# Layer 2 of a four-layer image kernel: high and low parts in the layout of the images, columns reordered by the evictions, another order of steps

## The chip, the cores and the metric

The kernel runs on one core of one Trainium2 chip. The metric is the time of one execution on the device, in microseconds (us). Before the change three runs took 6418.2, 6427.65 and 6427.76 us, so the median is 6427.65 us.

## The reference

The input is a batch of 32 images with 96 channels of 56 x 56. Four layers follow each other, and each adds its result to its input. Every layer first normalises its input over groups of three channels (`_gn`). The change lies in layer 2, a block with weights and activations rounded to four bits:

```python
def _L2_conv_ref(x, w1, ..., v3):
    h = bn(conv(x, quant_w(w1, BITW), b1, 1, 0, 1), g1, be1, m1, v1)      # 96 -> 576 channels, 1x1
    h = act_q(h, BITA)                                                    # clip to [0, 1], round to 15ths
    h = bn(conv(h, quant_w(w2, BITW), b2, 1, 1, HID), g2, be2, m2, v2)    # 3x3 in each channel
    h = act_q(h, BITA)
    h = bn(conv(h, quant_w(w3, BITW), b3, 1, 0, 1), g3, be3, m3, v3)      # 576 -> 96 channels, 1x1
    return x + h

x = x + _L2_conv_ref(_gn(x), ...)
```

The other layers are an inverted residual block with squeeze and excitation (layer 0), a wavelet convolution (layer 1) and a 9 x 9 convolution in each channel (layer 3). They aren't touched.

## The kernel before

**Layout.** Between the layers an image lies as 96 partitions (channels) with 3136 values each, in the order tile, phase, row, column: four tiles `t` of 14 rows; in each tile four phases `p`, which are the columns with the same remainder by 4; then 14 rows, then 14 columns `q`. Two images share one buffer `pair`, so an image `xt` is read in runs of 14 values (56 bytes) with a gap after each. Layers 1 and 3 work in this layout. Layer 2's 3x3 convolution needs columns that are neighbours to lie beside each other ("natural" order).

**Work of one image in layer 2.** The 576 hidden channels are five blocks `k` of 128 (the last one holds 64 channels, each in two halves). Each step has a letter, and the numbers after it are its arguments:

- `s`, `u`, `v`, `b`, `x` make the statistics and centre the image (VectorE, called DVE in the profile, and two tiny matmuls `pn` and `pv`).
- `h` (`high`, line 1011) writes `hi`, the normalised image in the rounded format that TensorE multiplies (F32R), on ScalarE (ACT). `l` (`low`, line 1017) writes `lo`, what that rounding left, on DVE. Both go from the layout of the phases to natural order, so they write one value in four: `h` once for each of four phases, `l` once for each of four phases in each of four tiles.
- `e` (`expand`, line 1039) multiplies block `k` of the first weights with tile `i` of `hi` and of `lo`: two halves of 392 columns, two matmuls each. The eviction (line 1029 on ACT, 1027 on DVE) scales the sum and writes it as whole numbers, `u`.
- `m` (`activate`, line 1048, DVE) clips `u` into the padded image `apad`.
- `a` (`depthwise`, line 1058) does the nine taps as matmuls of 64 x 64 with diagonal weights, four to an area of the array: 72 matmuls for each `k` and half image (36 for the last block). It fills two PSUM tiles (one for the last block). Their evictions (lines 1029 and 1027) put the columns back in the order of the phases.
- `n` (line 1048, DVE) clips, `j` (`project`, line 1095) multiplies with the third weights, `d` (line 1102, DVE) adds to the image, `o` takes the statistics for layer 3 and stores the images.
- `r` (line 1022, DVE) prepares the sum with the input.

**Order.** The queues of TensorE (PE), DVE and ACT are in program order, which is written out by hand: `run_steps` goes through the string `L2_ORDER` once for each image, and a `+` or `-` after a step means the next image or the one before. `L2_ON_DVE` names the evictions that go to DVE: `e00` is `expand` for `k` = 0, `i` = 0, and `a301` is the second PSUM tile of `depthwise` for `k` = 3, first half. In the order before, an image's expansions, mixed with the projections of the image before it, are followed by all of its depthwise steps. The issue of DMAs on SP and the one power on POOL (line 989) are not ordered by hand.

**Buffers.** All sums of layer 2, `ps`, `pn`, `pv`, `psd` and `psj`, are tiles of one pool with four buffers of two PSUM banks each. `hi` and `lo` have one buffer, `u` three. Three pairs of images are held; after the second image of a pair, `store` writes it to `y2` and `fetch` loads the next pair from `y1` into its place, 112 bytes to a packet.

Of the kernel before, what the change touches and what calls it, by code (L numbers as in the profile page):

```python
# [12 lines left out]
F32R = mybir.dt.float32r  # L13
I16 = mybir.dt.int16
AF = mybir.ActivationFunctionType
ALU = mybir.AluOpType
# [4 lines left out]
B, C, H, W = 32, 96, 56, 56  # L21
# [4 lines left out]
RT = 7  # L26
NT = RT * W
W2 = W // 2
NPH = 4
W4 = W // NPH  # L30
HH = H // 2
PH = HH * NPH
NP = H // (2 * RT)
# [31 lines left out]
    z1 t28 c0 a2  # L65
"""
L2_ORDER = """
    e00 e10 e11 e12 l3 j0- d0- e01 e20 e02 e21 r u+ e03 e13 j1- m0 e22 d1- e30 m1 e40 v+ j2- d2- e31
    e41 e23 b+ e42 j3- x+ e32 e33 m2 d3- m3 s++ e43 h0+ m4 a00 a10 o- a11 n1 a01 a20 h1+ a30 a21 l0+
    a31 n0 a40 l1+ n2 l2+ a41 n3 n4  # L70
"""
L2_ON_DVE = {"e00", "e20", "a301", "a201"}


class Shared:
# [843 lines left out]
def layer2(ctx, tc, S, k2, y1, y2, norm3):  # L919
# [9 lines left out]
    nc = tc.nc  # L929
    cp = ctx.enter_context(tc.tile_pool(name="l2d", bufs=1))  # L930
    pool = ctx.enter_context(tc.tile_pool(name="l2", bufs=1))
# [4 lines left out]
    CC, HALF, N9 = NBLK - 1, 64, 2 * NBLK - 1  # L936
    w1, w3, diag, s1, o1, s2, o2, s3, o3 = k2.constants
# [59 lines left out]

        nc.vector.tensor_scalar(im["xt"], im["xt"], im["gm"], None, ALU.subtract)

    def natural(t, p):  # L1000

        return t.rearrange("c (t r) (q p) -> c p t r q", t=NP, p=NPH)[:, p]

    def phase(im, p):
        return im["xt"].rearrange("c (t p r) q -> c p t r q", t=NP, p=NPH)[:, p]

    def high(im, half):
        if half == 0:
            im["hi"] = pool.tile([C, H, W], F32R, tag="hi", name="hi")
        for p in (2 * half, 2 * half + 1):  # L1010
            nc.scalar.activation(natural(im["hi"], p), phase(im, p), AF.Copy, scale=im["rstd"])  # L1011

    def low(im, i):
        if i == 0:
            im["lo"] = pool.tile([C, H, W], F32R, tag="lo", name="lo")
        for p in range(NPH):
            nc.vector.scalar_tensor_tensor(natural(im["lo"], p)[:, i], phase(im, p)[:, i], im["rstd"],
                                           natural(im["hi"], p)[:, i], ALU.mult, ALU.subtract)

    def residual(im):  # L1020

# [2 lines left out]
    def evict(out, ps, s, o, c, on_dve):  # L1024

        if on_dve:
            nc.vector.tensor_scalar(out, ps, s[:, c : c + 1], o[:, c : c + 1], ALU.mult, ALU.add)
        else:
            nc.scalar.activation(out, ps, AF.Identity, bias=o[:, c : c + 1], scale=s[:, c : c + 1])  # L1029

    def expand(im, k, i):

        if i == 0:
            im["u"][k] = up.tile([128, HW], I16, tag="u", name="u")
        ps = psum.tile([128, 2, 512], F32, tag="mm", name="ps")
        for j in range(2):
            r0 = (2 * i + j) * RT
            for part in ("hi", "lo"):
                nc.tensor.matmul(  # L1039
                    ps[:, j, :NT], w1[:, k * 128 : k * 128 + 128],  # L1040
                    im[part][:, r0 : r0 + RT, :].rearrange("c h w -> c (h w)"),
                    start=(part == "hi"), stop=(part == "lo"),
                )
        evict(im["u"][k][:, 2 * i * NT : 2 * (i + 1) * NT].rearrange("p (j n) -> p j n", j=2), ps[:, :, :NT],
              s1, o1, k if k < CC else N9 - 1, f"e{k}{i}" in L2_ON_DVE)

    def clip(out, u):
        nc.vector.tensor_scalar(out, u, 0.0, 15.0, ALU.max, ALU.min)
# [12 lines left out]
    def depthwise(im, k, h):  # L1061
# [21 lines left out]
        for x, (n, p, c) in enumerate(parts):  # L1083
            evict(u[:, 2 * n * NT : 2 * (n + 1) * NT].rearrange("p (m j x) -> p j m x", j=2, m=NPH),
                  p[:, :, :NT].rearrange("p j (x m) -> p j m x", m=NPH), s2, o2, c, f"a{k}{h}{x}" in L2_ON_DVE)

# [20 lines left out]
    def store(im):  # L1107
# [7 lines left out]
    step = {  # L1115
        "s": stats, "u": group_mean, "v": group_variance, "b": residual_factors, "x": centre,
        "h": high, "l": low, "r": residual, "e": expand, "m": activate, "a": depthwise, "n": activate2,
        "j": project, "d": add, "o": store,
    }
# [115 lines left out]
def kernel_body(tc, w, x, out):  # L1235
    nc = tc.nc
    with ExitStack() as ctx:
# [33 lines left out]
        with ExitStack() as ctx2:  # L1271
            k2 = Layer2(ctx2, tc, S, w, y1)

            def behind(pair):
                k2.prepare(pair)
                if not k2.stages:
                    k2.begin(min(2 * pair, C - GR))

            layer1(tc, w, y0, norm1, t1, t2, t3, y1, behind)
            k2.begin(C)  # L1280
            layer2(tc, S, k2, y1, y2, norm3)
# [122 lines left out]
```

## Time and profile before

| | |
|---|---|
| median of three runs | 6427.65 us |
| the profiled execution: time, span | 6420.77 us, 6419.0 us |
| clock of TensorE granted, mean | 0.975 |
| layer 2, first expansion to last projection | 4212.2 to 5949.6 us |
| busy in that stretch: PE, DVE, ACT | 1620, 1207, 1213 of 1737 us |
| DMA issues in layer 2 | 392 KB each, six to a pair of images and direction |

How to read it. The profile is of one execution. A busy time is the sum of an engine's instructions. In the tables of groups a row has the line of the code, the engine, the operation, what it writes and reads with shapes, the count, and then busy time in us, the mean of one in ns, and the idle time before it with what ended it. In a timeline the columns are start in us, duration in us, engine, line, operation, and in brackets how long the engine had been idle and what released it; "issue" means that nothing in the profile explains it. In the table of waits a row ends with the time in total, the number of waits and the longest.

### The profile page before, as it was taken

The numbers are of one execution on the slowest core, as the hardware profiler recorded it, in microseconds if no ns is written. First come the engines' busy times: TensorE is split into PE (matmuls) and PEld (weight loads), VectorE is DVE, ScalarE is ACT, GpSimd is POOL, SyncE is SP. The second block draws the span as 40 slices with busy tenths as digits, with TensorE's granted clock in tenths as the row PEclk, the third lists the DMA queues.
The fourth block names the chain that finished last, engine by engine and source line by source line (L and its number), as shares of the span: only waits on it lengthen the run. The fifth ranks groups of instructions, "written<-read, shape, count | busy, mean of one in ns | idle before, by whom it ended". The sixth has DMA issues, their size and how long they took to land.

```text
span 6419.0 us, 115759 instructions
## 1 busy us (share of the span) xinstructions
PE 6013.8 (94%) x49064; PEld 3571.1 (56%) x49064; DVE 5173.8 (81%) x5533; ACT 4052.9 (63%) x5716; POOL 223.1 (3%) x157
## 2 busy tenths in 40 slices
PE   4999999999999999999969999989999999999699
PEld 2444444444444444444435666668777777777344
DVE  6999999999999999999947666667676766776587
ACT  4676666766766667667535566567676766766355
POOL 4000000000000000000000000000000000000000
PEclk8999999999999999999979999999999999999899
DMA  3022221222211222113365866558787686964988
GB/s 95 6 48 53 45 46 32 49 55 47 42 32 43 54 49 42 32 37 40 23 86 142 150 148 146 130 30 54 39 53 41 51 43 44 51 42 29 174 254 245
DMA packets 1305765, 452.95 MB, mean 71 GB/s; under 512 B 1123151, under 2 KB 1301063, under 8 KB 1303327
## 3 DMA queue, kind: packets, MB, share of 16 engines
q1 hardware_dynamic: 1305246, 445.54, 47.5%
q8 instruction: 386, 6.32, 0.5%
q14 instruction: 133, 1.08, 0.1%
HBM read 284.44 MB, written 214.08 MB: 78 GB/s over the span
## 4 chain that ended last, share of the span: by engine, by line
PE 76%; ACT 13%; DVE 5%; DMA 3%; issue 2%; POOL 1%; SPq 1%; ACTq 0%; DVEq 0%; POOLq 0%
PE psd L388 18%; PE psd L1058 11%; PE ps L335 11%; PE ps L1039 6%; PE pc L774 6%; PE pc L1210 5%; PE psj L447 5%; ACT junk L287 4%; DVE h L360 4%; PE psj L1095 3%; ACT hi L1011 2%; ACT hpad L347 2%; PE pc L758 2%; ACT a L1029 2%; PE psj L448 2%
## 5 line engine op out<-in xcount | busy, mean ns | idle before, releaser
L360 DVE SCALAR_TENSOR_TENSOR h<-hpad,l_wdw,h 128x3136 f32<-128x3136 f32 x768 | 2662.6, 3481 | 40.7 <-ACT h L355 26.8
L1058 PE MATMUL psd<-apad,diag 64*64 64x392 bf16 x20736 | 930.3, 332 | 117.1 <-issue 62.4
L335 PE MATMUL ps<-xn,l_wexp 96*128 96x392 f32 x2560 | 894.5, 501 | 32.6 <-ACT xn L321 31.5
L1058 PEld LDWEIGHTS <-diag 64*64 64x64 bf16 x20736 | 699.3, 107 | 343.7 <-issue 170.3
L388 PE MATMUL psd<-hpad,diag 64*64 64x392 f32 x9216 | 831.1, 511 | 0.0
L347 ACT ACTIVATE hpad<-ps,o,s 128x784 f32<-128x784 f32 x512 | 546.6, 1082 | 305.0 <-PE ps L335 301.8
L335 PEld LDWEIGHTS ps<-xn,l_wexp 96*128 96x128 f32 x2560 | 479.4, 191 | 401.7 <-issue 37.3
L604 ACT COPY T<-raw 32x112 f32<-32x112 f32 (+2 forms) x1440 | 462.8, 384 | 300.4 <-DMA raw<-tdiff 216.8
L1029 ACT ACTIVATE u<-ps,o,s 128x784 int16<-128x784 f32 x576 | 536.9, 1003 | 160.6 <-PE ps L1039 141.7
L1029 ACT ACTIVATE a<-psd,o,s 128x784 int16<-128x784 f32 x448 | 424.6, 1000 | 322.2 <-PE psd L1058 322.2
L447 PE MATMUL psj<-h,wg 128*96 128x392 f32 x1536 | 606.7, 531 | 15.3 <-ACT hpad L347 7.7
L388 PEld LDWEIGHTS psd<-hpad,diag 64*64 64x64 f32 x9216 | 346.9, 131 | 467.9 <-issue 433.3
L1039 PE MATMUL ps<-hi,l_w1q 96*128 96x392 f32 x1280 | 462.5, 361 | 9.3 <-ACT hi L1011 9.2
L1210 PE MATMUL pc<-x,T 128*112 128x416 f32 (+1 forms) x1152 | 415.4, 523 | 41.8 <-DMA X<-y 40.6
L774 PE MATMUL pc<-x,T 128*112 128x416 f32 (+1 forms) x1152 | 444.3, 522 | 0.0
L1039 PE MATMUL ps<-lo,l_w1q 96*128 96x392 f32 x1280 | 438.0, 342 | 0.0
L388 PE MATMUL psd<-hhalf,diag 64*64 64x392 f32 x4608 | 417.6, 510 | 0.0
L447 PEld LDWEIGHTS psj<-h,wg 128*96 128x96 f32 x1536 | 248.5, 166 | 284.4 <-issue 250.2
L347 ACT ACTIVATE hhalf<-ps,o,s 64x56 f32<-64x56 f32 (+1 forms) x192 | 163.7, 852 | 340.1 <-PE ps L335 338.3
L1210 PEld LDWEIGHTS pc<-x,T 128*112 128x112 f32 x1152 | 204.1, 178 | 252.6 <-issue 234.3
L366 ACT ACTIVATE hab<-psd,o,s 128x392 f32<-128x392 f32 x256 | 170.9, 672 | 254.3 <-PE psd L388 254.3
L388 PEld LDWEIGHTS psd<-hhalf,diag 64*64 64x64 f32 x4608 | 182.7, 132 | 222.9 <-issue 222.6
(209 smaller groups left out, 7653.1 us busy)
## 6 DMA issues: line engine op xcount, KB each, us to landing
X<-y SPq DMA_DIRECT2D x192, 392.0 KB
y<-xt SPq DMA_DIRECT2D x180, 392.0 KB
xt<-in_x_dram SPq DMA_DIRECT2D x16, 2352.0 KB
y<-y SPq DMA_DIRECT2D x96, 392.0 KB
xt<-y SPq DMA_DIRECT2D x96, 392.0 KB
out_dram<-y SPq DMA_DIRECT2D x96, 392.0 KB
twav<-zwav SPq DMA_DIRECT2D x768, 36.8 KB
raw<-twav SPq DMA_DIRECT2D x96, 168.0 KB
```

What stands on the lines that cost most here:

```text
L287: nc.scalar.activation(junk, im["xt"][:, i * 2 * RT * NPH : (i + 1) * 2 * RT * NPH], func, bias=bias, accum_out=im[name][:, i : i + 1])
L335: nc.tensor.matmul(ps[:, j, :NT], wexp[:, k * 128 : k * 128 + 128], im["xn"][:, j, rows, :].rearrange("c h w -> c (h w)"), start=True, sto ...
L347: nc.scalar.activation(window(im["pad"][k][p], p.stop - (p.start or 0), 0, 0, r0, n).rearrange("p r (w j) -> p j r w", j=2), ps[p, :, :NT] ...
L360: nc.vector.scalar_tensor_tensor(h2, window(im["pad"][k], 128, t // 3 - 1, t % 3 - 1, 0, H), wdw[:, k, t : t + 1], h2, ALU.mult, ALU.add,)
L388: nc.tensor.matmul(ps[c * HALF : (c + 1) * HALF, j, :NT].rearrange("p (r q m) -> p r q m", q=W4, m=2), diag[p, k - AB, t, :], phases(v[:, ...
L447: nc.tensor.matmul(out, wg[:, k, :], phases(im["h2"][k][:, rows], j), start=(k == 0), stop=False)
L604: nc.scalar.copy(to.rearrange("x t (p s) -> x t p s", p=NPH), v[:, k])
L774: nc.tensor.matmul(ps[:PH, to], st["T"][j][:, h, k, :], st["x"][:, j, h, of], start=False, stop=(n == NK - 1))
L1029: nc.scalar.activation(out, ps, AF.Identity, bias=o[:, c : c + 1], scale=s[:, c : c + 1])
L1039: nc.tensor.matmul(ps[:, j, :NT], w1[:, k * 128 : k * 128 + 128], im[part][:, r0 : r0 + RT, :].rearrange("c h w -> c (h w)"), start=(part ...
L1058: nc.tensor.matmul(ps[q, j, :NT].rearrange("p (r w) -> p r w", w=W), diag[p, k, t, :], v, start=(t == 0), stop=(t == 8))
L1210: nc.tensor.matmul(ps[:, :, to], st["T"][:, h, k, :], st["x"][:, h, :, of], start=(n == 0), stop=(n == NK - 1))
```

## The change

`hi` and `lo` now lie in the layout of the images. `high` is one activation for each half image (two tiles), and `low` one operation for each tile, both with writes in order. The expansion's matmuls read, for each half of a tile, the four phases of seven rows: four runs of 98 values. So the sums in PSUM lie phase by phase, and the eviction of an expansion reads them in steps of 98 values and writes `u` in natural order. The depthwise part and all that follows it keep their shapes.

The order of steps is a new one. Eight more evictions go to DVE: it has two of the expansions' and two of the depthwise ones before, and eight and four after. `h` and `l` keep their names but are fewer instructions: `h0`, `h1` are halves, `l0` to `l3` are tiles as before.

```diff
 L2_ORDER = """
-    e00 e10 e11 e12 l3 j0- d0- e01 e20 e02 e21 r u+ e03 e13 j1- m0 e22 d1- e30 m1 e40 v+ j2- d2- e31
-    e41 e23 b+ e42 j3- x+ e32 e33 m2 d3- m3 s++ e43 h0+ m4 a00 a10 o- a11 n1 a01 a20 h1+ a30 a21 l0+
-    a31 n0 a40 l1+ n2 l2+ a41 n3 n4
+    a10- m4- a21- h1 a31- l0 l1 l2 a11- a40- l3 a41- r- n2- n3- n1- e30 e20 u+ e10 n0- e31 e21 e11
+    e22 n4- e32 e12 e33 v+ m3 e23 j0- e40 d0- m2 e13 b+ e41 e00 e42 e01 e02 j1- d1- j2- e03 d2- m0
+    j3- e43 d3- a20 x+ a30 m1 a00 h0+ o- a01 s++
 """
-L2_ON_DVE = {"e00", "e20", "a301", "a201"}
+L2_ON_DVE = """
+    a000 a201 a211 a301 e01 e03 e12 e22 e31 e41 e42 e43
+""".split()
...
-    def high(im, half):
-        if half == 0:
-            im["hi"] = pool.tile([C, H, W], F32R, tag="hi", name="hi")
-        for p in (2 * half, 2 * half + 1):
-            nc.scalar.activation(natural(im["hi"], p), phase(im, p), AF.Copy, scale=im["rstd"])
+    ROWS = 2 * RT * NPH
+    def high(im, i):
+        if i == 0:
+            im["hi"] = pool.tile([C, H * NPH, W4], F32R, tag="hi", name="hi")
+        rows = slice(2 * i * ROWS, 2 * (i + 1) * ROWS)
+        nc.scalar.activation(im["hi"][:, rows], im["xt"][:, rows], AF.Copy, scale=im["rstd"])
     def low(im, i):
...
-        for p in range(NPH):
-            nc.vector.scalar_tensor_tensor(natural(im["lo"], p)[:, i], phase(im, p)[:, i], im["rstd"],
-                                           natural(im["hi"], p)[:, i], ALU.mult, ALU.subtract)
+        rows = slice(i * ROWS, (i + 1) * ROWS)
+        nc.vector.scalar_tensor_tensor(im["lo"][:, rows], im["xt"][:, rows], im["rstd"], im["hi"][:, rows],
+                                       ALU.mult, ALU.subtract)
...
         for j in range(2):
-            r0 = (2 * i + j) * RT
             for part in ("hi", "lo"):
+                v = im[part].rearrange("c (t p r) q -> c t p (r q)", t=NP, p=NPH)
                 nc.tensor.matmul(
-                    ps[:, j, :NT], w1[:, k * 128 : k * 128 + 128],
-                    im[part][:, r0 : r0 + RT, :].rearrange("c h w -> c (h w)"),
-                    start=(part == "hi"), stop=(part == "lo"),
+                    ps[:, j, :NT].rearrange("p (m x) -> p m x", m=NPH), w1[:, k * 128 : k * 128 + 128],
+                    v[:, i, :, j * RT * W4 : (j + 1) * RT * W4], start=(part == "hi"), stop=(part == "lo"),
                 )
-        evict(im["u"][k][:, 2 * i * NT : 2 * (i + 1) * NT].rearrange("p (j n) -> p j n", j=2), ps[:, :, :NT],
-              s1, o1, k if k < CC else N9 - 1, f"e{k}{i}" in L2_ON_DVE)
+        evict(im["u"][k][:, 2 * i * NT : 2 * (i + 1) * NT].rearrange("p (j x m) -> p j x m", j=2, m=NPH),
+              ps[:, :, :NT].rearrange("p j (m x) -> p j x m", m=NPH), s1, o1, k if k < CC else N9 - 1, f"e{k}{i}" in L2_ON_DVE)
```

In the new order an image's depthwise steps are split over two rounds of the string: `a20`, `a30`, `a00`, `a01` end one round, and `a10-`, `a21-`, `a31-`, `a11-`, `a40-`, `a41-` begin the next. On TensorE they still follow each other without other work between them. `h1` and the four `l` stand in that second part.

More of the change, by code (lines that the diff above doesn't have):

```diff
@@ L998, in centre @@
         nc.vector.tensor_scalar(im["xt"], im["xt"], im["gm"], None, ALU.subtract)
[L1000 to L1005, printed above, removed]
-    def high(im, half):
-        if half == 0:
-            im["hi"] = pool.tile([C, H, W], F32R, tag="hi", name="hi")
-        for p in (2 * half, 2 * half + 1):
-            nc.scalar.activation(natural(im["hi"], p), phase(im, p), AF.Copy, scale=im["rstd"])
+    ROWS = 2 * RT * NPH
[4 more added lines that the diff above has]
+        nc.scalar.activation(im["hi"][:, rows], im["xt"][:, rows], AF.Copy, scale=im["rstd"])
     def low(im, i):
         if i == 0:
-            im["lo"] = pool.tile([C, H, W], F32R, tag="lo", name="lo")
-        for p in range(NPH):
-            nc.vector.scalar_tensor_tensor(natural(im["lo"], p)[:, i], phase(im, p)[:, i], im["rstd"],
-                                           natural(im["hi"], p)[:, i], ALU.mult, ALU.subtract)
+            im["lo"] = pool.tile([C, H * NPH, W4], F32R, tag="lo", name="lo")
+        rows = slice(i * ROWS, (i + 1) * ROWS)
+        nc.vector.scalar_tensor_tensor(im["lo"][:, rows], im["xt"][:, rows], im["rstd"], im["hi"][:, rows],
+                                       ALU.mult, ALU.subtract)
     def residual(im):
```

## The prediction

> **What bounds the kernel now.** The profiled execution took 6420.77 us, 6419.0 of them span. The table of busy time by engine comes first, then the waits of TensorE within layer 2 (4212 to 5903 us), then TensorE's timeline, one image after another.
>
> ```profile
> PE 6013.8 (94%) x49064; PEld 3571.1 (56%) x49064; DVE 5173.8 (81%) x5533; ACT 4052.9 (63%) x5716; POOL 223.1 (3%) x157
> ```
> ```profile
> PE psd L1058 <- issue: 53.8, 36, 4.1
> PE psd L1058 <- ACT a L1029: 51.4, 52, 1.8
> ```
> ```profile
> 4281.68 28.10 PE L1058 MATMUL psd<-apad,diag 64*64 64x392 bf16 x648
> ```
> ```profile
> 4654.78 15.55 PE L1058 MATMUL psd<-apad,diag 64*64 64x392 bf16 x352
> 4671.03 3.74 PE L1058 MATMUL psd<-apad,diag 64*64 64x392 bf16 x82 [0.69 <-issue]
> 4676.61 3.24 PE L1058 MATMUL psd<-apad,diag 64*64 64x392 bf16 x70 [1.84 <-ACT a L1029]
> 4680.80 0.35 PE L1058 MATMUL psd<-apad,diag 64*64 64x392 bf16 x2 [0.95 <-ACT a L1029]
> 4681.69 3.24 PE L1058 MATMUL psd<-apad,diag 64*64 64x392 bf16 x70 [0.54 <-ACT a L1029]
> 4685.89 3.24 PE L1058 MATMUL psd<-apad,diag 64*64 64x392 bf16 x72 [0.95 <-ACT a L1029]
> ```
>
> TensorE is the bound, and an image has two stretches. The depthwise stretch (648 matmuls, steps `a`) takes 28.0 us when nothing holds it, as at 4281.68. The stretch of expansions and projections (120 matmuls) takes 21.47 us in every steady image, without a gap. So the floor is 49.5 us an image. Read off the timeline, the 32 depthwise stretches last 1045 us, 149 more than 32 x 28.0. That excess is all that the change can win in steady state.
>
> It has two causes. **13 stretches** show the four waits on ACT of the second fence and lose 5.1 us each to them: 13 x 5.1 = 66 us. The other 83 us are "issue" waits, in the middle of an accumulation group, 128 matmuls apart (in one image after 180 and 308). They end when the instruction queue (q8 on the page) delivers a 16 KB packet: the packet at 4616.8 took 2.2 us and TensorE, idle since 4615.4, resumed at 4619.5. Such a packet takes 0.9 to 1.1 us while no data moves or y2 is stored, and 2.0 to 2.4 us while y1 is loaded.
>
> Why the ACT waits, and why in alternate images? In the built program each PSUM tile waits for the eviction of an earlier one. With four buffers this is nearly always the fourth tile before. In exactly 13 images of before it is, for the last five tiles of the depthwise stretch, the third and then the second before (the buffer of `a20`'s second tile, which DVE evicts, is passed over). A wait on the second tile before exposes a whole eviction.
>
> [...] by the step of ACT's writes for 784 elements: 0.95 us in order, 1.10 at 8 bytes, 1.74 (median) at 16:
>
> ```profile
> L287 ACT ACTIVATE junk<-xt,nm 96x784 bf16<-96x784 f32 x128 | 121.5, 949 | 142.0 <-DVE nm L302 137.9 <-DVE s L233 1.0
> L321 ACT ACTIVATE xn<-xt,nb,rstd 96x784 f32<-96x784 f32 x128 | 129.6, 1098 | 29.0 <-DVE nb L312 29.0
> L1011 ACT ACTIVATE hi<-xt,rstd 96x784 fp32r<-96x784 f32 x128 | 214.1, 1788 | 32.2 <-DVE xt L998 32.2
> ```
>
> [...] The new matmuls still write PSUM in order; only evictions read it in steps. For those the trace shows no penalty: `a`, which already reads every fourth element, costs what `u` does, which reads in order, on both engines:
>
> ```profile
> L1029 ACT ACTIVATE u<-ps,o,s 128x784 int16<-128x784 f32 x576 | 536.9, 1003 | 160.6 <-PE ps L1039 141.7 <-DVE a2c L1048 19.0
> L1029 ACT ACTIVATE a<-psd,o,s 128x784 int16<-128x784 f32 x448 | 424.6, 1000 | 322.2 <-PE psd L1058 322.2
> L1027 DVE TENSOR_SCALAR a<-psd,s,o 128x784 int16<-128x784 f32 x64 | 70.0, 1094 | 209.0 <-PE psd L1058 209.0
> L1027 DVE TENSOR_SCALAR u<-ps,s,o 128x784 int16<-128x784 f32 x64 | 69.8, 1091 | 9.6 <-PE ps L1039 9.6
> ```
>
> [...] The trace has the blocks (256 instructions, 128 weight loads with 128 matmuls), but 83 us are not hidden. [...]
>
> **The change, part by part** (per image).
>
> *hi.* Four writes in 16-byte steps become two of 1568 elements in order. [...] ACT: 6.7 (214.1/32) to 3.2 us.
>
> *lo.* 16 of 196 elements (262.9/32 = 8.2 us) become 4 of 784. The same operation took 617 ns for 392 elements (L1102) and 3481 for 3136 (L360): 1.04 ns an element and 0.21 fixed, so 1.03 each. DVE: 8.2 to 4.1 us.
>
> *Evictions.* 8 more go to DVE (6 `u`, 2 `a`): 8 x 1.09 = +8.7 us on DVE, 8 x 1.0 off ACT. Sums: ACT's busy time in layer 2 (1212.7 us, 37.9 an image) falls by 11.5 to 26.4; DVE's (1207.0, 37.7) rises by 4.6 to 42.3. Both stay under 49.5.
>
> *Reordered columns.* PSUM read in steps of 98 elements, four at a time: not in the trace. I take 1.0 and 1.09 us, from `a`. Bounds: nothing gained, and twice that (as ACT's 16-byte writes cost against writes in order). Matmuls that read four runs of 98 instead of 392 in a row: from nothing to 4 ns each (the depthwise ones read seven runs at 173 ns, against 166 for the projections'), so up to 80 x 4 ns x 32 = 10 us. I take nothing.
>
> *New order, PSUM.* In the built program of after, no wait reaches back two tiles. In 13 images three waits of the depthwise stretch reach back three (`a11`'s second tile, both of `a4`). Only the first is exposed, by one eviction: 1.0 us. So 66 us become 13: **-53 us**.
>
> *New order, DVE.* I walked it tile by tile with these durations. In the expansion stretch DVE has seven `u`, three adds (`d`), the clips `n` and three `m` in a row, some 17 us of work, and waits for TensorE or ACT for most of the other 5. `d2` ends 21.1 us after the stretch begins, and `a20` needs its buffer at 21.2; `d3` ends at 24.1 and `a30` needs it at 24.3. In the depthwise stretch the two statistics (8.4 us) stand between `a000` and `a211`; `a211` ends about 1 us before its buffer is wanted. So nothing waits, but the margin is 0.1 us twice: **+5 us** for slips (0.15 x 32). Bounds 0 and 16.
>
> *ACT's queue.* `h0+` stands behind `a001`, `h1` behind `a210`, each before the next tile ends: hidden by 3.1 us of depthwise matmuls, even at 3.3 us.
>
> *SP, POOL.* Their sequences are the same. `o-` moves to the end, but its DMAs wait only for the last add, and that stands where it stood, three us later in the stretch. Store and load hold the DMA engines 81 us (4444 to 4525); a load is wanted by its statistics about 110 us after the store's issue and ends 91 us after it (4434 to 4525).
>
> *Fetching.* The same instructions are fetched. Y1's loads still cover one depthwise stretch of two, so those waits stay. In the 13 other images the ACT waits gave the fetcher time: **+8 us** (20 us in the first 20 us of 28).
>
> *Ends of the layer.* The first expansion follows after two `hi` of 1.6 us instead of four of 1.5, and its evictions use two engines: **-3 us** of 18.85. The end is as it was.
>
> Sum: -53 + 5 + 8 - 3 = -43, so 6378 us against the profiled 6420.8. The three runs are 6418.2 to 6427.8; from about 6424, near their middle, I forecast **6380 us**.
>
> **Rivals.**
> 1. *Fetching stays as it is or eases* (no +8 and no slips, -56; at best the single wait of 13 us is hidden and fetching eases by 6, -75): 6350 to 6368. For it: several loaded stretches show no wait (27.99 us at 5037). Against it: denser matmuls ask for blocks sooner. Chance 0.2.
> 2. *Fetching takes the gain back.* Without ACT's waits TensorE arrives at the next missing block: 83 becomes 125 or more, and -2 to -12 us remain, about 6417. For it: in images with two fetch waits ACT's came on top. Chance 0.08.
> 3. *DVE becomes the bound: slower.* If reading PSUM in steps of 98 costs DVE twice, 8 `u` are 0.8 to 1.1 us longer each. The 5 us that DVE is idle in the expansion stretch take most of 7 x 0.9; `d2` and `d3` are then 2 to 4 us late in every image, and so are `a20` and `a30`: +64 to +128 - 43, about 6470. It decides from 1.3 us of delay an image. Against it: the four rows above. Chance 0.1.
> 4. *hi and lo don't get faster* because the reads in runs of 14 remain. L287 reads the same runs at 0.95 us; and the order hides 3.3 us. Part of the main case.
>
> **How the numbers follow.** Main case 0.62: 6355 to 6410. With rival 1 faster to 6345 and rival 2 up to 6425, the range 6345 to 6425 leaves out rival 3 and the tails. A measurement tells 0.2% (13 us) from no change: faster 0.82, the same 0.08, slower 0.10.
>
> **What would show it.** `hi` x64 at 1.6 us, `lo` x128 at 1.03, `u` at 1.00 and 1.09; TensorE's wait on ACT near 13 us instead of 51; depthwise stretches of 28.0 to 29 us beside stores and 30 to 34 beside loads; expansion stretches of 21.5. I am wrong if these grow past 22 us, if waits on DVE appear before `a20` or `a30`, or if "issue" waits exceed 110 us.

## The result, and the profile after

The kernel after takes **6398.39 us** (median of seven runs, 6382.0 to 6408.35) where before takes 6427.65 beside it. The ratio is 0.9955, with a 95% interval of 0.9941 to 0.9968. A second group of runs, on its own comparison with before, gave 0.9964 (0.9948 to 0.998). So the change saves about 0.4%: 29 us by the medians of the first group, 21 by those of the second. The forecast was 6380 us.

The profiled execution of after took 6408.35 us (span 6406.5), the slowest of its seven. It is therefore read stage by stage, and not by its total.

First the row of busy time, then TensorE's waits inside layer 2 (4213 to 5884 us). A row of waits ends with total, number and longest. `psd` are the sums of the depthwise part, `a` what their evictions write.

```profile
PE 6023.8 (94%) x49064; PEld 3530.5 (55%) x49064; DVE 5295.7 (83%) x5405; ACT 3730.4 (58%) x5396; POOL 221.1 (3%) x157
```
```profile
PE psd L1055 <- issue: 64.2, 53, 4.7
PE psd L1055 <- ACT a L1027: 12.1, 13, 0.9
```

The 52 waits on ACT have become 13, one in each of 13 images. TensorE's timeline shows a stretch without a wait, and one of the 13:

```profile
4287.30 27.67 PE L1055 MATMUL psd<-apad,diag 64*64 64x392 bf16 x648
...
4651.00 21.83 PE L1055 MATMUL psd<-apad,diag 64*64 64x392 bf16 x506
4673.76 6.29 PE L1055 MATMUL psd<-apad,diag 64*64 64x392 bf16 x142 [0.92 <-ACT a L1027]
```

The 32 depthwise stretches, from their first matmul to the next expansion, now take 996.8 us together (1045.2 before). An expansion stretch takes **22.0 us, and took 21.47**. Two groups of rows belong to this. The first has the work that became cheaper and the evictions (count, then busy us, mean ns, idle before):

```profile
L1027 ACT ACTIVATE u<-ps,o,s 128x784 int16<-128x784 f32 x384 | 369.5, 1001 | 136.3 <-PE ps L1037 136.0 <-DVE apad L1045 0.2
...
L1025 DVE TENSOR_SCALAR u<-ps,s,o 128x784 int16<-128x784 f32 x256 | 276.6, 1091 | 100.9 <-PE ps L1037 96.1
...
L1015 DVE SCALAR_TENSOR_TENSOR lo<-xt,rstd,hi 96x784 fp32r<-96x784 f32 x128 | 123.4, 1023 | 0.0
...
L1009 ACT ACTIVATE hi<-xt,rstd 96x1568 fp32r<-96x1568 f32 x64 | 101.9, 1593 | 33.7 <-DVE xt L1000 33.7
```

`hi` and `lo` cost 1.59 and 1.02 us; the 1.6 that the prediction counts for `hi` was the author's estimate. The evictions that read PSUM in steps of 98 cost what those in order did, 1.00 and 1.09. The second group has the expansion's matmuls, of before and then of after, and explains the longer expansion stretch:

```profile
L1039 PE MATMUL ps<-hi,l_w1q 96*128 96x392 f32 x1280 | 462.5, 361 | 9.3 <-ACT hi L1011 9.2
...
L1039 PE MATMUL ps<-lo,l_w1q 96*128 96x392 f32 x1280 | 438.0, 342 | 0.0
```
```profile
L1037 PE MATMUL ps<-hi,l_w1q 96*128 96x392 f32 x1280 | 468.6, 366 | 4.8 <-ACT hi L1009 4.8
L1037 PE MATMUL ps<-lo,l_w1q 96*128 96x392 f32 x1280 | 447.3, 349 | 4.3 <-DVE lo L1015 2.5 <-issue 1.8
```

Matmuls overlap, so the mean is longer than the step from one start to the next. That step went from 179 to about 184.5 ns (medians), and 80 matmuls x 5.5 ns x 32 images is 14 us.

### The profile page after: what moved, and what is told of

Same layout as the page of the kernel before. It is cut to its first block, busy times and chain, and to the rows that moved or that the text cites. A ratio compares the mean times of both kernels' runs of the same rounds, so it can differ in the third digit from the quotient of the medians.

```text
span 6406.5 us, 115408 instructions
## 1 busy us (share of the span) xinstructions
PE 6023.8 (94%) x49064; PEld 3530.5 (55%) x49064; DVE 5295.7 (83%) x5405; ACT 3730.4 (58%) x5396; POOL 221.1 (3%) x157
## 4 chain that ended last, share of the span: by engine, by line
PE 78%; ACT 9%; DMA 5%; DVE 4%; issue 2%; SPq 2%; POOL 1%; ACTq 0%; DVEq 0%
PE psd L390 19%; PE psd L1055 14%; PE ps L337 11%; PE ps L1037 8%; PE pc L776 6%; PE psj L449 5%; ACT junk L289 4%; PE psj L1092 3%; DVE h L362 3%; DMA raw<-tdiff 2%; ACT hpad L349 2%; PE pc L760 2%; PE pc L1207 2%; PE psj L450 2%; PE pa L734 1%
## 5 line engine op out<-in xcount | busy, mean ns | idle before, releaser
L1055 PEld LDWEIGHTS <-diag 64*64 64x64 bf16 x20736 | 642.1, 107 | 352.4 <-issue 119.2
L1027 ACT ACTIVATE a<-psd,o,s 128x784 int16<-128x784 f32 x384 | 372.0, 1002 | 654.6 <-PE psd L1055 654.6
L1027 ACT ACTIVATE u<-ps,o,s 128x784 int16<-128x784 f32 x384 | 369.5, 1001 | 136.3 <-PE ps L1037 136.0
L1025 DVE TENSOR_SCALAR u<-ps,s,o 128x784 int16<-128x784 f32 x256 | 276.6, 1091 | 100.9 <-PE ps L1037 96.1
```

The lines of the kernel that those rows point to most:

```text
L1055: nc.tensor.matmul(ps[q, j, :NT].rearrange("p (r w) -> p r w", w=W), diag[p, k, t, :], v, start=(t == 0), stop=(t == 8))
```

## The experiments

Two theories stood against each other. **A**: the gain comes from the order in which PSUM buffers come free, and the new layout of `hi` and `lo` only makes room on DVE and ACT. **B**: the gain comes from the cheaper `hi` and `lo`.

All times are medians; each group of runs has its own runs of before, and the ratio to those is what counts. "Depthwise" is the sum of the 32 stretches in the profiled execution. "Rest" is that sum less 32 undisturbed stretches (28.0 us in before, e4 and e7, 27.6 in the others) and less the ACT waits of the 13 stretches where there are any (66 us of time between starts in before, 10 in e7, 16 elsewhere). What is left are mainly the "issue" waits. It also holds matmuls that ran at a granted clock of 0.5, which cost 13 us in before and in after (3 to 17 in the other rows), and about 0.3 us for each wait that lies between the starts of two matmuls but not in the wait itself.

| kernel | ratio to before (95%) | depthwise | expansion stretch | rest |
|---|---|---|---|---|
| before | 1 | 1045 | 21.47 | 83 |
| after | 0.9955 (0.9941 to 0.9968) | 997 | 22.0 | 98 |
| e1 new order, old layout | 1.014 (1.0123 to 1.0156) | 1021 | 25.9 median | - |
| e2 new layout, old order | 1.0008 (0.9999 to 1.0018) | 1020 | 21.94 | - |
| e3 after, contiguous reads | 0.9943 (0.9926 to 0.996) | 1003 | 21.52 | 104 |
| e4 before, one eviction moved | 0.9926 (0.9914 to 0.9938) | 965 | 21.47 | 53 |
| e5 after again | 0.9964 (0.9948 to 0.998) | 999 | 22.0 | 100 |
| e6 after, one eviction moved | 0.9933 (0.9916 to 0.995) | 980 | 22.0 | 97 |
| e7 before, two evictions moved | 0.9932 (0.9913 to 0.995) | 984 | 21.47 | 78 |
| e8 old order, contiguous, none on DVE | 0.9905 (0.9888 to 0.9921) | 970 | 21.47 | 86 |
| e9 after without loads | 0.9853 (0.9836 to 0.9871) | 926 | 22.0 | 43 |
| e11 e3 and e6 together | 0.9921 (0.9899 to 0.9942) | 973 | 21.54 | 90 |

**e1: the order without the layout.** The kernel before, with `L2_ORDER` and `L2_ON_DVE` of after.

> The new order of steps and the new set of evictions on DVE, but hi and lo in natural order as before (four writes of ACT per half image, sixteen of DVE), and expansions that read 392 columns in a row. Theory A (the order is what removes ACT's waits, the layout pays for the order's DVE work and costs TensorE 0.5 us per expansion stretch): expansion matmuls are back at 179 ns start to start, 21.5 us per stretch (-16 us), but DVE carries 4.1 us more per image, 46.4 of 49.5 us, and ACT 3.5 us more; clips and adds come late, TensorE waits for DVE or hi/lo 1 to 3 us in every image: +32 to +96, in all 6415 to 6480 us. Rival B (the layout is needed for nothing, the order alone brings the gain): no such waits, 6398 - 16 = about 6382 us. In both the ACT waits of 13 images are about 1 us each, as in after.

It took 6487.66 us, 1.4% or 88 us longer than before, so A's direction, and more than its range, which ended 52 us above before. The waits of its expansions show the place:

```profile
PE ps L1039 <- DVE gm L979: 60.9, 26, 4.0
...
PE psd L1058 <- ACT a L1029: 21.3, 13, 2.0
...
PE ps L1039 <- ACT hi L1011: 9.2, 1, 9.2
```

In 26 images the expansions wait on average 2.3 us until DVE has read the group means, because 16 writes of `lo` (602 ns each) make DVE's queue longer. The waits are only part of it. After one of them:

```profile
4888.41 0.45 PE L1039 MATMUL ps<-hi,l_w1q 96*128 96x392 f32 x1 [3.29 <-DVE gm L979]
...
4889.24 0.34 PE L1039 MATMUL ps<-hi,l_w1q 96*128 96x392 f32 x1
4889.42 0.34 PE L1039 MATMUL ps<-lo,l_w1q 96*128 96x392 f32 x1
...
4890.20 0.53 PE L1039 MATMUL ps<-hi,l_w1q 96*128 96x392 f32 x1
4890.53 0.53 PE L1039 MATMUL ps<-lo,l_w1q 96*128 96x392 f32 x1
```

The starts are 0.18 us apart, and then 0.33 until 4892.8: the granted clock of TensorE was 0.51 in that stretch. It fell to 0.5 like this 17 times in e1's expansions, for 3.4 or 6.8 us, and not once in those of before (where only the first image begins at 0.5, up to 4230.9 us). The expansion stretches take 113 us more than in before; 64 us of that are waits and about 43 the lower clock, together about 1.7 times what the table of waits says. The new order needs the new layout.

**e2: the layout without the order.**

```diff
 # the kernel after, with the string and the set of before
-    a10- m4- a21- h1 a31- l0 l1 l2 a11- ...
+    e00 e10 e11 e12 l3 j0- d0- e01 e20 ...
-L2_ON_DVE = """
-    a000 a201 a211 a301 e01 e03 e12 e22 e31 e41 e42 e43
-""".split()
+L2_ON_DVE = {"a201", "a301", "e00", "e20"}
```

> The new layout of hi and lo and the new evictions, with the order of steps and the DVE set of before. In its built program 13 images again have PSUM waits that reach back 3, 2, 2, 2, 2 tiles at the end of the depthwise stretch. Theory A (those waits come from the order of the buffers): the 66 us stay within 10, the four-run matmuls add 16 us, so 6428 + 16 - 0 to 10: 6434 to 6444 us, slower than before. Rival B (the gain came from cheaper hi and lo, 11.5 us of ACT less per image): the waits shrink to under 20 us, and the time is 6398 or less.

It took 6404.7 us where before took 6399.27: no gain. B falls.

```profile
PE psd L1053 <- issue: 51.8, 48, 4.2
PE psd L1053 <- ACT a L1025: 44.0, 52, 1.1
```

There are again 52 waits on ACT, as in before, and 44.0 us of them against 51.4. Cheaper `hi` shortens each a little and removes none. Of the 25 us that the depthwise part loses (1045 to 1020), the four-run matmuls take 15 back in the expansions (21.47 to 21.94, 31 times), and the total shows no gain.

**e3: contiguous reads.** Each matmul takes two whole phases of a tile instead of seven rows of four phases. The eviction then steps across both banks.

```diff
-                v = im[part].rearrange("c (t p r) q -> c t p (r q)", t=NP, p=NPH)
+                v = im[part][:, (2 * i + j) * ROWS // 2 : (2 * i + j + 1) * ROWS // 2]
...
-              ps[:, :, :NT].rearrange("p j (m x) -> p j x m", m=NPH), ...
+              ps[:, :, :NT].rearrange("p j (m x) -> p x j m", m=2), ...
```

> As after, but each expansion matmul reads 392 values in a row (two whole phases of a tile, 14 rows) instead of four runs of 98, and the eviction puts them in order (it reads PSUM in steps of 196 across both banks and still writes in order). The same result is computed. Theory A (four runs cost the matmul 5 to 6 ns): start to start 179 ns, expansion stretches 21.5 instead of 22.0 us, 6398 - 16 = 6382 us, if the evictions still take 1.00 and 1.09 us. Rival B (the 5 ns come from evictions that read PSUM in steps beside the matmuls): stretches stay at 22.0, time 6398. Rival C: an eviction that alternates between two banks costs more, 1.1 us or above; then waits on ACT or DVE in the expansion stretch, above 6398.

```profile
L1037 PE MATMUL ps<-hi,l_w1q 96*128 96x392 f32 x1280 | 460.3, 360 | 4.8 <-ACT hi L1009 4.8
L1037 PE MATMUL ps<-lo,l_w1q 96*128 96x392 f32 x1280 | 438.0, 342 | 2.9 <-DVE lo L1015 2.5 <-issue 0.4
...
L1027 ACT ACTIVATE u<-ps,o,s 128x784 int16<-128x784 f32 x384 | 369.0, 1002 | 120.9 <-PE ps L1037 120.7 <-DVE apad L1045 0.2
```

The matmuls are back at 360 and 342 ns, the stretches at 21.5 us, and the eviction still costs 1.00 us. So the moving operand's pattern costs the 0.5 us, and not the PSUM reads. In the total the interval (0.9926 to 0.996) overlaps that of after, so the gain of 15 us is shown in the stretches, and only likely in the total.

**e4: one eviction.** The smallest edit that tests A.

```diff
 # the kernel before
-L2_ON_DVE = {"e00", "e20", "a301", "a201"}
+L2_ON_DVE = {"a301", "e00", "e20"}
```

> Before, with a single edit: the eviction of a20's second PSUM tile goes to ACT instead of DVE. In the built program 13 images then have waits that reach back 3, 3, 3 tiles (as in after) in place of 3, 2, 2, 2, 2. Theory A (the order in which PSUM buffers come free made 66 us of ACT waits): they become about 13, so -53, less 8 to 14 us of fetch waits that no longer hide: 6428 - 39 to 53 = 6375 to 6389 us, as good as or better than after. Rival B (ACT was late because of its load, hi above all, which this edit leaves and raises by 1 us per image): no gain, 6428 us or above.

It took 6350.95 us where before took 6399.27: 0.9926, more gain than the whole change gives.

```profile
PE psd L1058 <- issue: 38.5, 46, 3.3
...
PE psd L1058 <- ACT a L1029: 11.1, 12, 0.9
```

ACT's waits go from 51.4 to 11.1 us although ACT has an eviction more per image. A holds. What the new order of steps is worth apart from the set of evictions on DVE wasn't measured, since e1 and e2 change both together; e4 shows that the set alone is enough.

**e5 and e6: after again, and after with `a211` on ACT.**

> The kernel after, unchanged, beside the others of this group, so that they are compared on one chip. On the first pair of measurements it was 0.9955 of before; the same is expected: 0.994 to 0.997.

> After, with a single edit: the eviction of a21's second PSUM tile goes to ACT instead of DVE. In the built program every wait of the depthwise stretches then reaches back four tiles or more (in after, 13 images have 3, 3, 3 at the end). Theory A (the buffers' order): the 13 waits of 0.9 us on ACT in the trace vanish, -12 to -16 us, ratio to before 0.9930 to 0.9937. Rival B (ACT gets too much: h1 and two evictions in a row): new waits on ACT, no gain, 0.9955 or above. Rival C (fetching takes it back): the waits vanish, issue waits grow by as much, 0.9955.

e5 gave 0.9964, as expected. In e6 no wait of a depthwise stretch on ACT is left in the list of waits, and the stretches sum to 980 us, 19 less than in e5. The ratio, 0.9933, is where A put it. The intervals of e5 and e6 just overlap at 0.995, so the gain is shown in the waits and the stretches, and only likely in the total.

**e7: both evictions.** The kernel before with `L2_ON_DVE = {"e00", "e20"}`.

> Before, with both depthwise evictions that DVE has (a20's and a30's second tiles) on ACT. In the built program all waits of all 32 depthwise stretches reach back four tiles. Theory A: beside the experiment with one eviction (0.9926) another 12 us go, ratio about 0.991, 6340 us where before takes 6399. Rival B: ACT now has 18 evictions and 6.7 us of hi in a stretch of 28 us, 24.7 us in all; if hi ahead of an eviction makes it late, TensorE waits on ACT 1 us or more in most images, +32 us: 0.9945 or above.

It gave 0.9932, not the 0.991 of A. The timeline of a stretch shows why:

```profile
4285.97 21.99 PE L1058 MATMUL psd<-apad,diag 64*64 64x392 bf16 x506
4308.48 6.29 PE L1058 MATMUL psd<-apad,diag 64*64 64x392 bf16 x142 [0.52 <-ACT a L1029]
```

Every wait reaches back four tiles, and yet 13 stretches still have one wait on ACT, at the same place, of 0.5 instead of 0.9 us. ACT, with 18 evictions and 6.7 us of `hi` in a stretch of 28 us, is late by itself: `h1+` occupies it for 3.3 us from 4303.5, and four evictions follow without a pause. So this edit gains 6 us of the 16 that e4 left, and the times can't tell it from e4. Rival B was right in kind, in 13 images and not in most.

**e8: contiguous layout, old order, no depthwise eviction on DVE.**

> The new layout of hi and lo with matmuls that read 392 in a row (as in the experiment on contiguous reads), the order of steps of before, and no depthwise eviction on DVE. All waits of the depthwise stretches reach back four tiles. ACT has 3.5 us and DVE 4.1 us less per image than in the kernel with two evictions moved. Theory A (TensorE is the bound, so cheaper hi and lo beside it bring nothing once the buffers are in order): the same as the kernel with two evictions moved, within 10 us, ratio about 0.991; expansion stretches 21.5. Rival B (cheaper hi and lo are worth something by themselves): 0.989 or less.

It took 6346.25 us beside e5's 6388.7 and before's 6409.5: 0.9905, the fastest of all. The undisturbed stretch is 27.59 us, and one wait on ACT is left:

```profile
PE psd L1053 <- issue: 59.5, 65, 3.8
...
PE psd L1053 <- ACT a L1025: 1.3, 1, 1.3
```

So cheap `hi` is worth something in the old order: it leaves ACT the room for two more evictions, which e7 lacks. Against e7 the stretches of 13 images lose the wait of 0.5 us, and all are 0.4 us shorter. In the total the intervals of e7 and e8 still overlap (0.9913 to 0.995, 0.9888 to 0.9921), so rival B's "worth something" is shown in the stretches alone; those of e8 and e5 don't.

**e9: no loads.** `fetch` in layer 2 issues no DMA after the third pair.

> After, without the loads of y1 into layer 2's image buffers except for the first three pairs: the later images are computed from what the buffers hold, so the values from layer 2 on are not the reference's; every other instruction, the stores of y2 among them, is as in after. Without the loads the built program has no 3, 3, 3 in the depthwise stretches. Theory A (y1's small packets slow the instruction fetch): fetch packets stay at 0.9 to 1.1 us, the depthwise stretches lose their issue waits (68 us in the trace of after) and the 13 waits on ACT, their sum falls from 997 to between 890 and 910 us, ratio to before about 0.982. Rival B (TensorE asks for instructions faster than the fetcher can bring them, whatever else moves, or the stores do it): at least 40 us of issue waits stay, ratio 0.987 or above.

```profile
PE psd L1055 <- issue: 31.1, 29, 2.9
```

The "issue" waits fall from 68.0 us (in the whole of after) to 31.1, and the ratio is 0.9853, both between the theories: half of the waits go with the loads. All but one that are left lie beside stores of `y2`. In the built program the three waits that reached back three tiles are gone as well: it is the loads that made the builder pass over the buffers that DVE frees. That they do so because DVE's statistics wait for them is argued, not tested.

**e10 and e12: what in the reads costs time, and no traffic at all.**

> After, with expansion matmuls whose 392 values come in one run for tile 0, in two of 196 for tile 1, four of 98 for tile 2 and fourteen of 28 for tile 3, all within the tile, so that the columns of tiles 0, 1 and 3 come out in a wrong order (values from layer 2 on are not the reference's); evictions as in after. Theory A (each further run costs the moving side some time): start to start 179, 181, 184.5 and about 203 ns, some 1.8 ns per further run. Rival B (any break costs the same once): 179, then 184 to 185 three times. Rival C (it is PSUM read in steps by the evictions): all four at 184 to 185.

> Two readings in one kernel, made from after; values from layer 2 on are not the reference's. (1) Expansion matmuls read their 392 values as one run that begins 8 bytes off a 16-byte boundary for tile 0, as 28 runs of 14 for tile 1, 7 runs of 56 for tile 2, 49 runs of 8 for tile 3. In the run before, 1, 2, 4 and 14 runs of 392, 196, 98 and 28 gave 180, 178.5, 184 and about 180 ns, so the number of runs is not what counts. Theory L [...]: about 182, 217 [...], 179 and 179 ns. Rival S (something particular to four runs of 98, such as their spacing of 784 bytes): 179 to 180 for all four. Rival M (a run that begins or ends off a boundary costs once per matmul): 184 for tiles 0 and 1. (2) In layer 2's steps no data moves: no loads of y1 after the first three pairs, and the stores of y2 all come after the last step (so the whole time is much longer and is not compared). Without loads alone, 31 us of issue waits were left in the depthwise stretches, all beside stores. Theory T (data traffic makes the instruction fetch late): they vanish, 32 stretches of 27.6 to 28 us, sum under 890. Rival F (TensorE outruns the fetcher by itself): 30 us or more are left.

Each ran once and only its trace is used. The steps from start to start (mean of the medians of a tile's `hi` and `lo` matmuls) were:

| runs x values (bytes) | 1 x 392 | 1 x 392, 8 bytes off | 2 x 196 (784) | 4 x 98 (392) | 7 x 56 (224) | 14 x 28 (112) | 28 x 14 (56) | 49 x 8 (32) |
|---|---|---|---|---|---|---|---|---|
| ns | 180 | 179.5 | 178.5 | 184 | 180.5 | 181 | 200 | 179 |

In the timeline of e12, tile 1's matmuls (28 x 14) are followed by another tile's:

```profile
4657.91 0.37 PE L1041 MATMUL ps<-lo,l_w1q 96*128 96x392 f32 x1
4658.11 0.37 PE L1041 MATMUL ps<-hi,l_w1q 96*128 96x392 f32 x1
4658.32 0.36 PE L1041 MATMUL ps<-lo,l_w1q 96*128 96x392 f32 x1
4658.52 0.34 PE L1041 MATMUL ps<-hi,l_w1q 96*128 96x392 f32 x1
4658.70 0.34 PE L1041 MATMUL ps<-lo,l_w1q 96*128 96x392 f32 x1
4658.89 0.34 PE L1041 MATMUL ps<-hi,l_w1q 96*128 96x392 f32 x1
```

The starts are 0.20 us apart, and then 0.18. All three theories of e10 fall. Of e12's, S and M fall and the figures of L hold in part: 28 x 14 costs more, but 200 ns and not 217, and the one run that begins 8 bytes off takes 179.5 and not 182. Only the two patterns whose runs are no whole multiple of 16 bytes (392 and 56 bytes) cost anything, 184 and 200 ns against 178.5 to 181. What the price follows exactly stays open.

For the second reading, one line of waits and one stretch:

```profile
PE psd L1059 <- issue: 5.5, 3, 2.5
```
```profile
4626.06 27.67 PE L1059 MATMUL psd<-apad,diag 64*64 64x392 bf16 x648
```

While no data moves (4250 to 5600 us), not one of the depthwise stretches has a wait; each takes 27.6 us. The sum is 892, just over the 890 that T allowed, with three longer stretches near the layer's two ends, where packets do move. Theory T holds: with traffic there are 68.0 us of "issue" waits (after), and without it none.

**e11: both edits to after.**

> After with two edits that were tried one by one: matmuls that read 392 in a row, and a21's second eviction on ACT. If they add up: 0.9964 - 0.0025 (four-run reads) - 0.002 to 0.003 (three waits in 13 images), ratio 0.991 to 0.992, the same as the order of before with the contiguous layout (0.9905). Rival (the new order is worth something of its own): 0.989 or less. Other rival (the fetch waits take one of them back): 0.994.

It gave 0.9921, as if they add up, but the interval (0.9899 to 0.9942) excludes only the first rival, and that by a hair; the other stays open. With the same reads the old order (e8) does at least as well, 0.9905.

## Why the prediction was right, and where it was off

**The floor.** Right in kind: TensorE is the bound, and with no traffic its depthwise stretches have no wait (e12, 4250 to 5600 us). It was 0.4 us too high in the depthwise stretch. In 28 of the 32 stretches of before a matmul starts 0.4 us late after matmul 146; matmuls overlap, so the timeline shows one unbroken row. The 0.4 us need the old `hi` and the old order together: in before `h0+` holds ACT for 3.5 us from 4283.0, right ahead of the first evictions. An undisturbed stretch takes 27.6 us with the cheaper `hi` in the old order (e2, e8), and also with the old `hi` in the new order (e1). 0.4 x 32 = 13 us were gained for which the prediction counted nothing.

**ACT's waits, -53.** Right. 13 stretches lost 5.1 us each and now lose 1.2: -50. e4 shows the mechanism by itself: the position of one eviction in the order of the buffers.

**Slips of DVE, +5.** No wait on DVE appeared before `a20` or `a30`. Nor did rival 3 come true: the evictions stayed at 1.09 us on DVE. Long waits for DVE, image after image, are in e1 alone, with the old `lo`, and there inside the expansions.

**Fetching, +8.** The rest grew from 83 to 98 us, so +15. Each figure is from one profile, and the table has 43 to 104 from kernel to kernel; five kernels with the new order and y1's loads have 90 to 104, those with the old one 53 to 86 (e4's 53 comes from the fastest of its six executions, 20 us under their median). So how much of the 15 the change makes is open.

The mechanism was right in its first half. By the profile's times all 57 "issue" waits of after, and all 29 of e9, end 1.2 to 2.5 us after a 16 KB packet of the instruction queue has landed; a random moment of these traces does so in 15 of 100 cases. In one stretch of after these waits stand behind 214, 342, 470 and 598 matmuls, 128 apart. The lag is longer than most of the waits, so the packet has often landed before the wait begins. (The packet that the prediction puts at 4616.8 begins at 4615.2 in the trace, takes 2.4 us and has landed 2.0 us before TensorE resumes.)

The second half, that y1's loads make the packets slow, isn't enough. Without the loads no packet between 4300 and 5700 us took longer than 1.5 us, and 31.1 us of waits remained. Those packets begin late. In e9, two packets of one stretch between which TensorE doesn't wait begin 5.3 us apart (median of 57, at most 6.2) while no other packet moves, and 6.7 us apart (median of 26, at most 9.9) beside stores, though they take 0.9 to 1.4 us in both. In e12, with no traffic, the depthwise stretches go from packet to packet without a wait; with traffic, the same depthwise instructions cost 68.0 us in after. Why a packet begins late beside other traffic was not tested.

**Reordered columns, 0 for the matmuls.** This is the term that was mis-sized without a reason. The bound was 4 ns, the value taken 0, and the runs show 5 to 6 ns, some 15 us. The rows that it was taken from are the depthwise matmuls, which read another type (bf16) in runs of 112 bytes; the new runs have 392 bytes, which is no whole multiple of 16. In e10 and e12 the runs of 392 and 56 bytes took 184 and 200 ns, and one run that begins 8 bytes off 179.5. The evictions were sized right, at 1.00 and 1.09 us.

**Start of the layer, -3.** From the matmul `pv` of the first image to the first depthwise one it was 28.5 us before, and 27.5 and 27.1 in the two profiles of after: about -1. The first stretch itself grew (18.85 to 22.19 us), since it now begins after one part of `hi` and waits inside for `lo`.

**The end.** From the last projection to the end it took 469.6 us before, and 482.8 and 471.3 in the two profiles of after: the two executions of one kernel differ by more than e5's differs from before, so nothing here can be put down to the change.

So the sum of the prediction, -43, becomes -50 (ACT) - 13 (the floor) + 15 (fetching) + 15 (reads) - 1 = -34. In the profiles the time from `pv` to the last projection is 1747 us in before and 1716 and 1714 in after, so -31 and -33; the medians of the totals fell by 29 and 21. The main term was right for its reason. That the sum came within its range owes something to luck: three terms were off by 7 to 15 us, and the gain that wasn't counted hides a part of the costs that weren't.

## What to carry to other kernels

When TensorE waits for an eviction, first look how many tiles back the wait reaches in the built program: with four buffers a reach of two cost four waits, 5.1 us, in each of 13 images of before, and the cure was to give a single eviction to another engine (e4: ACT's waits went from 51.4 to 11.1 us). Loads far from the place can set that order, as e9 shows. A wait of TensorE can come with more than its length: in e1, 64 us of waits in the expansions came with 43 us of a granted clock of 0.5. When a layout is changed, size the reads of TensorE too: in these matmuls it paid to keep each run of the moving operand a whole multiple of 16 bytes (178.5 to 181 ns, against 184 and 200), and to let the eviction, which reads PSUM in order and in steps of 98 and 196 values at the same cost (1.00 us on ACT, 1.09 on DVE), put the columns in order.

## What was not expected of the hardware

- Matmuls with runs of 98 values cost 184 ns and with 28 runs of 14 values 200, against 178.5 to 181 for every other pattern that was measured, with runs of 32, 112, 224, 784 and 1568 bytes. One run that starts 8 bytes off took 179.5.
- An eviction that reads PSUM in steps of 196 values, alternating between two banks, costs ACT 1002 ns and DVE 1090, as in order.
- Data traffic of 112-byte packets, loads or stores, goes with 31 to 76 us of "issue" waits of TensorE in this layer's depthwise stretches (e9 and e1 are the ends); while no data moves there are none (e12). They end 1.2 to 2.5 us after a packet of instructions has landed, and beside stores these packets begin late rather than take long (e9: 6.7 us apart instead of 5.3, 0.9 to 1.4 us each in both).
- In e1 the granted clock fell to 0.5 for 3.4 or 6.8 us 17 times in expansion stretches that TensorE spent in part waiting; a matmul then took 0.33 us from start to start instead of 0.18.
